# Layer 0's bias sums: three folds by DMA, one product a unit, and VectorE in 2 of 16 evictions

## The chip, the cores and the metric

The kernel runs on one core of one Trainium2 chip. The metric is the device time of one execution in microseconds (us); lower is better. A core has a matrix engine (TensorE, PE in the profile; its weight loads are PEld), a vector engine (VectorE, DVE), an activation engine (ScalarE, ACT), a general engine (GpSimd, POOL) and a queue engine for transfers (SyncE, SP). They run side by side, each in the order of its own instructions, and wait for each other at semaphores. Transfers by DMA are issued from SP's queue, or from GpSimd's, which can also add what it moves to what is there.

## The reference

Four layers run one after the other on x of shape (2, 512, 32, 32), all in float32: a deformable attention with an MLP (layer 0), a linear attention (layer 1) and two full attentions (layers 2 and 3). The change concerns one part of layer 0, the bias of its attention. For each of 16 units (2 batches of 8 groups), each of 1024 queries and each of 64 sampled keys, a small network with 128 hidden channels turns the distance into one number:

```python
pos = grid_q[:, :, None, :] - grid_kv[:, None, :, :]
bias = jnp.sign(pos) * jnp.log1p(jnp.abs(pos))
bias = jax.nn.relu(bias @ cpb_w1 + cpb_b1)
bias = jax.nn.relu(bias @ cpb_w2 + cpb_b2)
bias = (bias @ cpb_w3 + cpb_b3).reshape(b, GROUPS, H * W, Hd * Wd)
sim = jnp.einsum('bhid,bhjd->bhij', qh, kh) + bias
attn = jax.nn.softmax(sim, axis=-1)
```

The last layer of the network is a sum over 128 channels, each weighted by an entry of cpb_w3. Since a positive factor can be moved inside the relu, the kernel scales the second layer's weights by the magnitudes of cpb_w3 and is left with a sum of channels with signs.

## The kernel before, in words

**The loop.** Layer 0 goes through `quads`: unit u (16), set of keys o (8) and half (2), 256 groups in all, numbered i. A group handles 4 keys. `first_hidden` (line 694) has VectorE make the first hidden layer of the next group, i + 1 (line 706). `second_hidden` (line 717) then handles group i in four quarters q of 32 channels. For each quarter, TensorE makes 32 channels of 4 keys on 128 partitions (line 730), so that partition 32k + r holds channel r of key k. ACT evicts it with relu and the bias `magb` (line 740). Quarter 0 holds the channels whose signs may differ from the rest's; ACT multiplies it by `flip` in a second pass (line 742).

**The sum over quarters.** Quarter 0 is added to quarter 1 by an accumulating DMA issued from GpSimd (line 747, 512 KB). GpSimd adds quarter 2 to quarter 3 (line 751). One group later, GpSimd adds the two sums (`join`, line 754, called at q == 1 of the next group's `second_hidden`).

**The folds.** What is left has 32 rows a key. After half 1, the tile `two` holds both halves of an o, and a DMA adds odd partitions to even ones (line 756, 512 KB): 16 rows a key. This goes with the join, one group after half 1. `refold` (line 762) folds a second time to 8 rows a key (line 766, 256 KB) and copies the 32 partitions left of each half into a `sum` tile by two DMAs on SP's queue (line 768, 128 KB each). It is due at group i + 2, where i is the group of half 1 (line 209), and is issued before quarter 3's eviction (line 738), so behind that group's join on GpSimd.

**The products.** Four sets o fill two `sum` tiles, and `sum_product` (line 783, matmul line 786) adds up their rows on TensorE against a matrix of signs into the scores `sim`. So there are two products a unit (`twice_product`, e = 0 and 1), one two sets after each four sets: behind group (u, 5, 1), and behind group (u + 1, 1, 1). There `attend` (line 805) starts for unit u: TensorE adds query times key to `sim` (line 812), and its later parts come one after each group. The end of the last unit has its own treatment (`last_set`), with fewer folds.

**Order and buffers.** PE, ACT, DVE and POOL run in the order in which the program writes the calls (`manual_schedule`, line 147); SP's queue isn't in that list. The quarters' PSUM tiles have 3 buffers (line 135), `two` and `sum` have 3 each (lines 626 to 630), quarters 0, 1 and 2 have 2, 3 and 2 (line 734). `load` (line 643) fetches tables `lb` for the first hidden layer on SP's queue.

Of the kernel before, what the change touches and what calls it, by code (L numbers as in the profile page):

```python
# [11 lines left out]
F32 = mybir.dt.float32  # L12
AF = mybir.ActivationFunctionType
# [22 lines left out]
    ("index", 1), ("row", 1), ("twelves", 8),  # L36
# [12 lines left out]
N_TWICE, N_FOLDED, N_SINGLE = 48, 56, 60  # L49
# [7 lines left out]
class Net:  # L57
# [40 lines left out]
    def layer0(self):  # L98
# [3 lines left out]
        with ExitStack() as ctx:  # L102
# [44 lines left out]
            with self.tc.manual_schedule(engines=engines):  # L147
# [39 lines left out]
                self.join, self.refolds, summed, group, sums = None, [], None, [], []  # L187
                for i, (u, o, half) in enumerate(quads):
# [9 lines left out]
                    last_set = i >= len(quads) - 8  # L198
                    if half == 0:
                        if i + 2 < len(quads):  # L200
                            both = self.two_tiles(f"h2_{u}_{o}3")
                            group.append([both[:, 0, :], both[:, 1, :], both])
                        else:
                            group.append([self.four_rows(f"h2_{u}_{o}{n}3") for n in range(2)])
                        if o % 4 < 2 and not last_set:
                            sums.append(self.four_rows(f"sum{u}_{o}"))
                    self.second_hidden(i, u, o, half, h1, group[-1], i + 1 == len(quads), last_set)
                    if half == 1 and not last_set:
                        self.refolds.append((i + 2, group[-1][2], sums[o % 2], o % 4 // 2))
                    if half == 1 and o % 4 == 1 and summed:  # L210
                        v, e, zs = summed
                        self.twice_product(v, e, zs, sims, ps_s)
                        summed = None
                        if e == 1:
                            if v == 8:
                                self.advance(after, lambda: False)
                                att = [apool.tile([P, N], F32, tag=f"att{t}", name=f"att{v}_{t}") for t in range(CT)]
                            self.advance(front, lambda: "v" in pairs[v // 2])
                            after.append(self.attend(v, pairs[v // 2], sims.pop(v), att, ps))
                            if v % 8 == 7:  # L220
                                after.append(self.projection(ps, att, ow, v // 8))
                    elif half == 1 and o % 4 == 3:
                        if last_set:
                            self.folded_product(u, o - 2, group[:2], sims)
                        else:
                            summed, group, sums = (u, o // 4, sums), [], []
# [5 lines left out]
                self.folded_product(u, o, group[2:3], sims)  # L232
# [35 lines left out]
    def sorted_weights(self, keep):  # L268
# [8 lines left out]
        self.places = self.spare[:, 3 * P : 4 * P + N_TWICE + N_FOLDED + N_SINGLE]  # L277
# [13 lines left out]
        many = keep.tile([P, 8], F32, tag="many", name="sort_many")  # L291
        vec.tensor_tensor(many, self.colr("twelves", 8), total.to_broadcast([P, 8]), ALU.is_le)
        vec.tensor_reduce(c["groups"], many, AX.X, ALU.add)
        vec.tensor_scalar(c["late"], c["groups"], 12.0, None, ALU.mult)
        vec.tensor_scalar(c["rest"], c["groups"], -12.0, 96.0, ALU.mult, ALU.add)
# [16 lines left out]
        signed = keep.tile([P, N_TWICE + N_FOLDED + N_SINGLE], F32, tag="signed", name="signed")  # L312
        pool.tensor_scalar(signed, self.places[:, P:], c["sign"], 1.0, ALU.mult, ALU.mult)
        self.twice = signed[:, 0:N_TWICE]
        self.folded = signed[:, N_TWICE : N_TWICE + N_FOLDED]
        self.single = signed[:, N_TWICE + N_FOLDED :]
# [15 lines left out]
        nc.scalar.copy(self.magb, small)  # L332
        self.flip = keep.tile([P, 1], F32, tag="flip", name="flip")
# [383 lines left out]
    def second_hidden(self, i, u, o, half, h1, one, final, last_set):  # L717
# [4 lines left out]
        nc = self.nc  # L722
        ys = []
        for q in range(4):
# [8 lines left out]
            if q < 3:  # L733
                y = self.hid2.tile([P, N], F32, tag=f"h2{q}", bufs=(2, 3, 2)[q], name=f"h2_{u}_{o}{half}{q}")
            else:
                y = one[half]
                if self.refolds and self.refolds[0][0] <= i:
                    self.refold(*self.refolds.pop(0)[1:])
            ys.append(y)
            nc.scalar.activation(y, hp, AF.Relu, bias=self.magb[:, q, 0:1])  # L740
            if q == 0:
                nc.scalar.activation(y, y, AF.Copy, scale=self.flip)  # L742
            elif q == 1:
                if final:
                    nc.vector.tensor_tensor(y, y, ys[0], ALU.add)
                else:
                    nc.gpsimd.dma_start(y, ys[0], accum_op=ALU.add)  # L747
                if self.join:
                    self.join(final)
            elif q == 3:  # L750
                (nc.vector if final else nc.gpsimd).tensor_tensor(y, y, ys[2], ALU.add)  # L751

        def join(final, z=ys[3], other=ys[1], fold=half == 1 and not final):
            (nc.vector if final else nc.gpsimd).tensor_tensor(z, z, other, ALU.add)  # L754
            if fold:
                nc.gpsimd.dma_start(one[2][0::2], one[2][1::2], accum_op=ALU.add)  # L756
                if last_set:
                    nc.sync.dma_start(one[0][1::2, :], one[1][0::2, :])
# [3 lines left out]
    def refold(self, both, to, second):  # L762


        nc = self.nc
        nc.gpsimd.dma_start(both[0::4], both[2::4], accum_op=ALU.add)  # L766
        for half in range(2):
            nc.sync.dma_start(to[2 * second + half :: 4, :], both[0::4, half, :])

    def twice_product(self, u, e, zs, sims, ps_s):  # L770

        if u not in sims:
            sims[u] = ps_s.tile([P, HF], F32, tag="sim", name=f"sim{u}")
        at = 16 - 16 * e
        self.sum_product(u, self.twice[:, at : at + 32], e == 0, zs, sims)

    def folded_product(self, u, o, group, sims):
        at = 24 - 4 * (o - o % 2)  # L780
        self.sum_product(u, self.folded[:, at : at + 32], False, [one[0] for one in group], sims)

    def sum_product(self, u, lhsT, start, zs, sims):
        for h in range(2):
            for jj, z in enumerate(zs):
                self.nc.tensor.matmul(
                    sims[u][h * NJ + jj * 32 : h * NJ + jj * 32 + 32, :],
# [1250 lines left out]
def _places():  # L2038

    q, row = np.arange(P) // 32, np.arange(P) % 32  # L2040
    got = np.zeros((P, P + N_TWICE + N_FOLDED + N_SINGLE), np.float32)
    got[:, :P] = np.where(q == 0, 96 + row, 12 * (row // 4) + 4 * (q - 1) + row % 4)
    p = np.arange(P)
    got[p, P + 16 + 8 * (p // 2 % 2) + 4 * (p % 2) + p // 32] = 1
    got[p, P + N_TWICE + 24 + 4 * (p % 2) + p // 32] = 1
    got[p, P + N_TWICE + N_FOLDED + 28 + p // 32] = 1
    return got


def _layout(i):  # L2050
# [10 lines left out]
    def over(v):  # L2061
        return np.broadcast_to(v.reshape(1, -1), (P, v.size))
# [12 lines left out]
        "row": (np.arange(P) % 32 // 4).astype(np.float32).reshape(P, 1), "twelves": over(np.arange(12, 108, 12, dtype=np.float32)),  # L2075
# [46 lines left out]
```

## Time and profile before

| | |
|---|---|
| median of 3 runs | 3221.99 us (3221.45 to 3223.23) |
| profiled execution, its own time | 3223.45 us |
| span from first to last instruction | 3221.7 us |
| granted TensorE clock, mean | 1.000 |
| PE busy | 3206.4 us (100%) |
| DVE busy | 2365.0 us (73%) |
| ACT busy | 1958.2 us (61%) |
| POOL busy | 2359.2 us (73%) |
| POOL DMA issues: line 747, 756, 766 | 255, 127, 124 |

All times of the profile are of one execution. A group line gives the line of the program, the engine and the operation, what it writes and reads by the program's names, the shape and the count; then busy time in us and the mean of one in ns; then the engine's idle time just before, and what ended it. Slices are fortieths of the span, each digit a share in tenths. In a timeline the columns are start, length, engine and line. "DMA to landing" is the time from a transfer's issue until its semaphore says that it has arrived. Layer 0's groups take about the first 1900 us.

### The profile page before, as it was taken

To read this page: it belongs to the slowest core of one execution; us is meant where nothing else is said; L and a number is where in the kernel's file an instruction comes from. 1 tells how busy PE (TensorE), PEld (TensorE's weight loads), DVE (VectorE), ACT (ScalarE), POOL (GpSimd) and SP (SyncE) were. 2 spreads that over 40 slices of the span, in tenths; PEclk is the share of its full clock that TensorE was granted. 3 is DMA by queue.
4 is the path that set the end of the run, shared out by engine and by line. 5 is a ranking of instruction groups with operands and counts; after the bars stand their busy time and mean duration, and the time that the engine had idled before them with its cause. 6 is when DMAs were issued, how large, how long until landed. Compare 5 with 4: busy or idle time off the path is not lost.

```text
span 3221.7 us, 58840 instructions
## 1 busy us (share of the span) xinstructions
PE 3206.4 (100%) x24188; PEld 1218.9 (38%) x24188; DVE 2365.0 (73%) x2746; ACT 1958.2 (61%) x2032; POOL 2359.2 (73%) x1558
## 2 busy tenths in 40 slices
PE   9999999999999999999999999999999999999999
PEld 4343333333333333333333334444555433455333
DVE  7778788778777778878777765475475689755897
ACT  7887887887886687887887752112231566213662
POOL 6999999999998699998999964442343458634575
PEclk9999999999999999999999999999999999999999
DMA  6787877787786577777787762111000000000001
GB/s 178 163 172 158 171 168 163 166 167 165 162 172 145 124 164 161 163 163 164 163 174 160 166 166 79 39 40 39 1 1 12 29 1 1 15 1 14 1 2 54
DMA packets 94350, 341.90 MB, mean 106 GB/s; under 512 B 16624, under 2 KB 18800, under 8 KB 78896
## 3 DMA queue, kind: packets, MB, share of 16 engines
q0 software_dynamic: 52832, 232.82, 37.4%
q1 hardware_dynamic: 40224, 103.06, 10.0%
q8 instruction: 195, 3.19, 0.4%
q10 hardware_dynamic: 1008, 2.08, 0.2%
q14 instruction: 91, 0.75, 0.1%
HBM read 67.36 MB, written 4.46 MB: 22 GB/s over the span
## 4 chain that ended last, share of the span: by engine, by line
PE 90%; DVE 5%; POOL 2%; DMA 1%; issue 1%; ACT 0%; DVEq 0%; SPq 0%; POOLq 0%; ACTq 0%
PE hp L730 52%; PE s L1659 5%; PE o L1688 5%; PE qk20P L1434 2%; PE qk30P L1434 2%; PE qk31P L1434 1%; PE m_7P L943 1%; PE m_6P L943 1%; PE m_4P L943 1%; PE m_3P L943 1%; PE m_0P L943 1%; PE qk21P L1434 1%; PE m_5P L943 1%; PE m_2P L943 1%; PE m_1P L943 1%; DVE sum L1675 1%
## 5 line engine op out<-in xcount | busy, mean ns | idle before, releaser
L730 PE MATMUL hp<-h,w2s 128*32 128x512 f32 x16384 | 1784.1, 593 | 0.2
L706 DVE CUSTOM_DVE_ANT_1 h<-tx,bank 128x1024 f32<-128x1024 f32 (+1 forms) x1028 | 1180.9, 1211 | 295.7 <-PE hp L730 197.6
L740 ACT ACTIVATE h<-hp,magb 128x1024 f32<-128x1024 f32 x1024 | 1131.2, 1109 | 359.6 <-PE hp L730 357.7
L730 PEld LDWEIGHTS hp<-h,w2s 128*32 128x32 f32 x16384 | 559.3, 110 | 1187.0 <-issue 1126.4
L754 POOL TENSOR_TENSOR h<-h,h 128x1024 f32<-128x1024 f32 x254 | 728.2, 2867 | 2.4 <-DMA h<-h 2.3
L751 POOL TENSOR_TENSOR h<-h,h 128x1024 f32<-128x1024 f32 x255 | 717.4, 2814 | 1.5 <-ACT h L740 1.5
L1663 ACT ACTIVATE e<-s 128x1024 f32<-128x1024 f32 x256 | 261.8, 1024 | 181.0 <-PE s L1659 176.5
L747 POOL DMA_DIRECT2D h<-h x255 | 275.4, 1080 | 99.6 <-ACT h L740 97.7
L742 ACT ACTIVATE h<-h,flip 128x1024 f32<-128x1024 f32 x256 | 295.0, 1152 | 8.4
L1688 PE MATMUL o<-e,v 64*64 64x512 f32 x2048 | 265.3, 590 | 2.1 <-DVE q L1727 2.1
L1659 PE MATMUL s<-q,k 64*64 64x512 f32 x2048 | 266.0, 591 | 0.0
L1670 POOL TENSOR_TENSOR some<-some,e 128x1024 f32<-128x1024 f32 x64 | 167.6, 2619 | 26.7 <-ACT e L1663 24.1
L1668 POOL TENSOR_TENSOR some<-e,e 128x1024 f32<-128x1024 f32 x32 | 76.1, 2377 | 141.4 <-DVE sum L1677 106.3
L766 POOL DMA_DIRECT2D h<-h x124 | 140.6, 1134 | 27.0 <-DMA h<-h 24.6
L1675 DVE TENSOR_TENSOR sum<-sum,e 128x1024 f32<-128x1024 f32 x64 | 124.0, 1937 | 29.5 <-ACT e L1663 26.8
L913 POOL TENSOR_TENSOR mlp_w<-mlp_w 128x512 f32<-128x512 f32 x16 | 24.2, 1514 | 160.4 <-DMA mlp_w<-in_mlp_w 96.0
L756 POOL DMA_DIRECT2D h<-h x127 | 109.1, 859 | 38.9 <-POOL h L754 37.2
L1688 PEld LDWEIGHTS o<-e,v 64*64 64x64 f32 x2048 | 77.9, 133 | 144.9 <-issue 135.1
L1659 PEld LDWEIGHTS s<-q,k 64*64 64x64 f32 x2048 | 76.5, 133 | 133.2 <-issue 117.2
L1009 ACT ACTIVATE mh<-mh,cols 128x512 f32<-128x512 f32 x64 | 46.0, 721 | 124.4 <-DVE mh L1027 64.3
L1422 POOL TENSOR_TENSOR sq<-q 128x512 f32<-128x512 f32 x32 | 33.2, 1039 | 98.0 <-DVE q L1441 54.3
L1673 DVE TENSOR_TENSOR sum<-e,e 128x1024 f32<-128x1024 f32 x32 | 80.8, 2524 | 32.0 <-ACT e L1663 32.0
(583 smaller groups left out, 3254.4 us busy)
## 6 DMA issues: line engine op xcount, KB each, us to landing
h<-h POOLq DMA_DIRECT2D x382, 512.0 KB, 5.6
lb<-logs SPq DMA_DIRECT2D x63, 512.0 KB, 6.5
h<-h POOLq DMA_DIRECT2D x124, 256.0 KB, 3.7
sum<-h SPq DMA_DIRECT2D x248, 128.0 KB, 3.5
mlp_w<-in_mlp_w SPq DMA_DIRECT2D x16, 1024.0 KB, 4.9
x<-in_x SPq DMA_DIRECT2D x8, 512.0 KB, 7.8
qkw<-in_l_qk SPq DMA_DIRECT2D x2, 2048.0 KB, 7.9
out<-x SPq DMA_DIRECT2D x15, 256.0 KB, 2.1
```

What stands on the lines that cost most here:

```text
L706: self.nc.vector._custom_dve(TENSOR_ADD_SAT, out=h1[r][:, k, cut, :], in0=x[:, 4 * half + 2 * r + k, :].unsqueeze(1).to_broadcast([P, H // ...
L730: nc.tensor.matmul(hp[rows, cut], lhsT=self.l0w2[:, 32 * q : 32 * q + 32], rhs=h1[k][:, cut], start=True, stop=True)
L740: nc.scalar.activation(y, hp, AF.Relu, bias=self.magb[:, q, 0:1])
L742: nc.scalar.activation(y, y, AF.Copy, scale=self.flip)
L747: nc.gpsimd.dma_start(y, ys[0], accum_op=ALU.add)
L751: (nc.vector if final else nc.gpsimd).tensor_tensor(y, y, ys[2], ALU.add)
L754: (nc.vector if final else nc.gpsimd).tensor_tensor(z, z, other, ALU.add)
L943: self.nc.tensor.matmul(acc[p], lhsT=w[:, a, k, p * P : (p + 1) * P], rhs=right(r, k), start=k == 0, stop=k == 1)
L1434: nc.tensor.matmul(acc, lhsT=left[0][a][:, c, t * P : (t + 1) * P], rhs=r[ri][:, c, :], start=c == 0, stop=c == 1)
L1659: nc.tensor.matmul(s[halves[c], par, :], lhsT=ks[p][rows, at : at + DH], rhs=qs[p][rows, cut], start=True, stop=True)
L1663: nc.scalar.activation(e, s, AF.Exp, scale=DH**-0.5)
L1688: nc.tensor.matmul(o[halves[par], r, :], lhsT=v[n // 2][rows, n % 2, at : at + DH], rhs=e[rows, par, :], start=(n == 0), stop=(n == NB - 1),)
```

## The change

- Units 0 to 14 fold a third time: a DMA adds rows 4::8 of `two` to rows 0::8 (16 partitions, 128 KB), leaving 4 rows a key. The two copies on SP's queue then take 16 partitions each (64 KB), and all eight sets of a unit share two `sum` tiles. There is one product a unit, with a new sign matrix `thrice`, at the place where the second one was: behind group (u + 1, 1, 1).
- `refold` becomes a generator. Its first step (the second fold) is due at group i + 2, its second (the third fold and the copies) one group later. `refold_more` makes due steps at q == 1, behind the join. The last unit folds twice, as before (`once`).
- The sorting of channels by sign goes in sets of 24 instead of 12, since the rows left of a key now hold 24 channels of the three last quarters and 8 of the first.
- In groups (3, 0) and (4, 1) of units 1 to 15 (`fused`), VectorE evicts quarter 2 and adds quarter 1 in one instruction: max with `under`, which is minus the bias, plus quarter 1. The bias left out there is added in quarter 0's second pass on ACT. The DMA now adds quarter 0 to quarter 2, after VectorE; GpSimd's addition of quarter 2 to quarter 3 is gone in these groups, and the join adds quarter 2.

```diff
@@ layer0
-                        if o % 4 < 2 and not last_set:
+                        if o < 2:
                             sums.append(self.four_rows(f"sum{u}_{o}"))
                     self.second_hidden(i, u, o, half, h1, group[-1], i + 1 == len(quads), last_set)
                     if half == 1 and not last_set:
-                        self.refolds.append((i + 2, group[-1][2], sums[o % 2], o % 4 // 2))
-                    if half == 1 and o % 4 == 1 and summed:
-                        v, e, zs = summed
-                        self.twice_product(v, e, zs, sims, ps_s)
-                        summed = None
...
+                        self.refolds.append([i + 2, self.refold(group[-1][2], sums[o % 2], o // 2, u == last)])
+                    if half == 1 and o == 1 and u > 0:
+                        v = u - 1
+                        sims[v] = ps_s.tile([P, HF], F32, tag="sim", name=f"sim{v}")
+                        self.sum_product(sims[v], self.thrice, True, before)
...
@@ sorted_weights
+        self.under = keep.tile([P, 1], F32, tag="under", name="under")
+        pool.tensor_scalar(self.under, self.magb[:, 2, 0:1], -1.0, 1.0, ALU.mult, ALU.mult)
@@ second_hidden
+        fused = u > 0 and (o, half) in ((3, 0), (4, 1)) and not final
...
             ys.append(y)
+            if q == 2 and fused:
+                vec.scalar_tensor_tensor(y, hp, self.under, ys[1], ALU.max, ALU.add)
+                pool.dma_start(y, ys[0], accum_op=ALU.add)
+                continue
             nc.scalar.activation(y, hp, AF.Relu, bias=self.magb[:, q, 0:1])
-            if q == 0:
+            if q == 0 and fused:
+                nc.scalar.activation(y, y, AF.Identity, scale=self.flip, bias=self.magb[:, 2, 0:1])
+            elif q == 0:
                 nc.scalar.activation(y, y, AF.Copy, scale=self.flip)
             elif q == 1:
...
-                else:
-                    nc.gpsimd.dma_start(y, ys[0], accum_op=ALU.add)
+                elif not fused:
+                    pool.dma_start(y, ys[0], accum_op=ALU.add)
                 if self.join:
                     self.join(final)
-            elif q == 3:
-                (nc.vector if final else nc.gpsimd).tensor_tensor(y, y, ys[2], ALU.add)
+                self.refold_more(i)
+            elif q == 3 and not fused:
+                (vec if final else pool).tensor_tensor(y, y, ys[2], ALU.add)
 
-        def join(final, z=ys[3], other=ys[1], fold=half == 1 and not final):
+        def join(final, z=ys[3], other=ys[2 if fused else 1], fold=half == 1 and not final):
...
-    def refold(self, both, to, second):
+    def refold_more(self, i):
+
+        going = []
+        for at, fold in self.refolds:
+            if at <= i:
+                for _ in fold:
+                    going.append((at + 1, fold))
+                    break
+            else:
+                going.append((at, fold))
+        self.refolds = going
+
+    def refold(self, both, to, c, once):
 
 
         nc = self.nc
         nc.gpsimd.dma_start(both[0::4], both[2::4], accum_op=ALU.add)
+        if not once:
+            yield
+            nc.gpsimd.dma_start(both[0::8], both[4::8], accum_op=ALU.add)
+        n = 4 if once else 8
         for half in range(2):
-            nc.sync.dma_start(to[2 * second + half :: 4, :], both[0::4, half, :])
+            nc.sync.dma_start(to[2 * c + half :: n, :], both[0::n, half, :])
```

## The prediction

> **What bounds the kernel now.** I read the page first: its slices, chain and groups.
>
> ```profile
> PE   9999999999999999999999999999999999999999
> POOL 6999999999998699998999964442343458634575
> PE 90%; DVE 5%; POOL 2%; DMA 1%; issue 1%; ACT 0%; DVEq 0%; SPq 0%; POOLq 0%; ACTq 0%
> L730 PE MATMUL hp<-h,w2s 128*32 128x512 f32 x16384 | 1784.1, 593 | 0.2
> L754 POOL TENSOR_TENSOR h<-h,h 128x1024 f32<-128x1024 f32 x254 | 728.2, 2867 | 2.4 <-DMA h<-h 2.3
> L751 POOL TENSOR_TENSOR h<-h,h 128x1024 f32<-128x1024 f32 x255 | 717.4, 2814 | 1.5 <-ACT h L740 1.5
> ```
>
> TensorE never rests: 0.2 us of idle time before 16384 matmuls. So one microsecond more or less of TensorE work or waiting in layer 0 is one microsecond of the kernel. GpSimd is the next fullest. Whatever ACT, VectorE or GpSimd are given or spared counts only if TensorE then waits. I write (u, o, half) for a group: unit u, key set o of 8, half 0 or 1; q is its quarter.
>
> So the next question is what TensorE's product L786 waits for, and how close that is. The answer for the copies' line L768 names it:
>
> ```profile
> L768 SPq DMA_DIRECT2D sum<-h x248: 458/524/2575, 60.1 to 1867.2; - x124
> ...
> who waited for it (us, times):
>   PEld sim L786: 1.4, 3
> ```
>
> Three of 31 products already wait a little for the copies of the folded sums. The margin is thin. Here is one product in order of time (start, length), the one at (u,1,1) that the change keeps; first TensorE, then GpSimd:
>
> ```profile
> 844.42 13.94 PE L730 MATMUL hp<-h,w2s 128*32 128x512 f32 x128
> 858.18 1.04 PE L786 MATMUL sim<-sum,signed 128*32 128x512 f32 x8
> ```
>
> ```profile
> 848.00 0.84 POOL L766 DMA_DIRECT2D h<-h  x1 [0.18 <-issue]
> 848.60 2.66 POOL L751 TENSOR_TENSOR h<-h,h 128x1024 f32<-128x1024 f32 x1
> 850.93 1.15 POOL L747 DMA_DIRECT2D h<-h  x1
> 851.54 2.97 POOL L754 TENSOR_TENSOR h<-h,h 128x1024 f32<-128x1024 f32 x1
> 854.81 0.86 POOL L756 DMA_DIRECT2D h<-h  x1 [0.29 <-POOL h L754]
> 857.75 1.14 POOL L747 DMA_DIRECT2D h<-h  x1
> ```
>
> The two groups (1,0) and (1,1) run from 844.4 to 858.2. The second fold L766 of the previous unit's o=7 goes out at 848.00, in the order written for (0,1). Asked for L766 and L768 in the stretches round it, the trace gives 3.4 us to landing for the fold, and for its two copies, issued from 851.50:
>
> ```profile
> DMA to landing us min/median/max: 3.0/3.7/4.4
> ```
>
> The second copy went out at 852.05 and took 4.4 us: the sums were whole at 856.4, 1.8 us before the product's place at 858.18.
>
> **What the Trainium skill says.** "DMA: Bandwidth & Descriptors", section "Queues, rings and completion order": descriptors are consumed in ring order on each DMA engine. So a fold issued straight behind another of the same queue waits for the other's data. The trace agrees as far as it goes: GpSimd's folds of 256 KB land after 3.7 us and those of 512 KB after 5.6 (medians), so more bytes ahead mean a later landing. Its section "Anatomy of one DMA — SWDGE (gpsimd) path" gives about 2.0 us fixed plus the bytes; this kernel's fastest fold took 3.2, so I use the trace. "TensorE: Matmul & The Clock Gate", section "Part 1: The HAM clock gate": TensorE falls to half rate after a free-running window of about 3.4 us without work, and needs about 3.4 us of work to come back. Here the longest gap before the end is 1.6 us, so no stretch of layer 0 shows it. The end of the trace does (columns: stretch, its length, busy time and count of PE, PEld, DVE, ACT and POOL, the clock, DMA share, GB/s):
>
> ```profile
> 3217.20:3219.90 2.70, 0.00 (x0) 0.00 (x0) 0.48 (x1) 0.00 (x0) 0.00 (x0) 1.00 0.56 188
> 3219.90:3221.70 1.80, 0.00 (x0) 0.00 (x0) 0.00 (x0) 0.00 (x0) 0.00 (x0) 0.50 0.02 7
> ```
>
> The clock is 0.50 from 2.7 us after the last matmul.
>
> **Part by part.**
>
> *Products.* Before, each unit ends in two products, after o=3 and after o=7. The change keeps one for units 0 to 14; unit 15 keeps what it had. The chain of waits shows 0.86 us for one (8 records at 858.36). Removed: 15 x 0.86 = 12.9 us of TensorE, on the path. **-12.9 us.**
>
> *The third fold, its issue.* 15 units x 8 = 120 more GpSimd DMAs. From the start of L747 at 850.93 to the next operation is 0.6 us; 8 x 0.6 = 4.8 us a unit. Removed from GpSimd: the q3 addition L751 in two groups of units 1 to 15, 2 x 2.8 = 5.6 us a unit. In the unit from 743.0 to 858.6 GpSimd is busy 107.5 of 115.6 us. It stays about there: 0 us, under TensorE's cover.
>
> *The third fold, its date.* This is the term that decides. The generator issues the second fold at group i+2 and the third, with the copies, at i+3, in both cases behind that group's join. For o=7 that is (1,0) of the next unit, and the product stays behind (1,1). In the stretch above, GpSimd reaches that point after L747, L754 and the first fold L756 of 854.81, thus at 854.81 + 0.6 = 855.4. TensorE's place for the product is 858.18: 2.8 us for a fold, a wake-up of SP and two copies. Now the price:
> - L756 of 854.81 landed after 4.4 us, at 859.3. The third fold is 128 KB behind it in the same queue. From 256 KB to 512 KB the stretch shows 3.4 and 4.4 us, so 0.5 us for 128 KB: 859.8. Low end: not held behind it, 3.2 us (the fastest L766) from 855.4: 858.6.
> - SP answers a landing in 0.1 us (landed 851.44, issued 851.50). Each copy is now 64 KB instead of 128. At 864.54 an undisturbed pair was whole 2.6 us after its first issue; the median pair takes 4.8 us. The bytes are half, but L747 of 857.75 moves its data then (it landed after 4.8 us). I take the middle, 3.6: 863.5.
> - So the product waits 863.5 - 858.2 = 5.3 us. Over the 15 products at this place the trace has 3.8 us on average from L756's issue to the product and 4.9 us to L756's landing: 4.9 + 0.5 + 0.1 + 3.6 - 3.8 = 5.3 again. Ends: 3.1 (no queueing, short copies) and 6.5 (median pair of before).
> TensorE issues in order, so attention's products of that unit and group (2,0) stand behind it. Nothing is won back: it had no idle time to give. 15 x 5.3 = **+79.5 us.**
>
> *The clock.* A gap of 5.3 us holds a whole free-running window of 3.4 us in (5.3 - 3.4)/3.4 = 0.56 of cases; the return at half rate costs half of 3.4 us. 0.56 x 1.7 x 15 = **+14 us**, an estimate from the skill's page; ends 0 and 15 x 1.7 = 25.
>
> *VectorE's eviction.* In (3,0) and (4,1) VectorE does max and add from PSUM. The nearest row is L375, also PSUM plus SBUF to 128x1024: 1.29 us, against ACT's 1.11 for the eviction it spares. Behind it on VectorE stands the next first hidden layer, 4.6 us of a 6.9 us group; the attention's steps leave VectorE nothing else in these two groups (one has the exponential on ACT, the other copies on ACT). TensorE needs the bank two quarters, 3.4 us, later. 0 us; if that cover is gone, up to 1 us x 30. The accumulating DMA now waits for VectorE instead of ACT's q1, some 1 to 2 us later; the join that needs it is a group later and may make GpSimd wait as long: within its slack.
>
> *The folded tiles.* There are three of `two`, and a tile of o is rewritten by q3 of (o+3,0). Copies whole at 863.5 stand against ACT's eviction near 867; over the trace the median time for the copies is 4.7 us and a fifth have under 3.5. ACT would then wait about 1 us, and TensorE has 2 us of spare banks. 0 us; bound +15.
>
> *SP.* The copies wait on SP's queue some 7 us longer. The loads of `lb` share it, but they go out a whole table (28 us) early. 0 us. Setup and `under`: below 0.5 us, taken as 0.
>
> Sum: -12.9 + 79.5 + 14 = +80.6 us on the profiled execution's 3223.45 us (span 3221.70, and 1.75 around it). That execution is 1.46 us over the median of 3221.99; on the median: 3222 + 81 = **3303 us**.
>
> **The rivals.**
> - *A short stall* (0.15). The third fold overtakes, the clock stays: 15 x 3.1 - 12.9 = +34, 3256 us. For it: small transfers have landed in 1.9 us. Against it: the fold goes out 0.6 us behind a 512 KB one.
> - *A long stall* (0.18). Copies no faster than now, clock down each time, tiles late: 15 x 6.5 + 25 + 15 - 12.9 = +125, 3347 us. For it: the copies' median is 3.5 us with a maximum of 11.3.
> - *The other side, sums in time* (0.04). Only the 12.9 us of products count: 3209 us. One mechanism: the third fold and its copies fit into the 2.8 us before the product. It decides where the chain from fold to last copy is under 2.8 us; from 3.7 us up even the saved product is lost. No fold of the trace lands under 3.2 alone. A still smaller chance (0.02) lies between.
>
> **How the numbers follow.** Main case 0.61 at 3303, with 3280 to 3330 as its own range; the rivals as above. The range of 3256 to 3345 leaves out some 2 in 10: the short stall's lower half, the long one's upper part, the other side. Faster by over 0.2% (6.4 us, about what a measurement can tell) 0.04, within 0.2% 0.02, slower 0.94.
>
> **What would show it.** TensorE's idle time before L786's successor in the new code should be 4 to 6 us in 15 places, put down to the copies sum<-h; the product's matmuls halve from 248 recorded to about 128. Matmuls after the gap should be slow for about 3 us if the clock falls. GpSimd's busy share should hold. I am wrong if the copies land before TensorE gets there, or if the waits on ACT or GpSimd grow beside the product.

## The result, and the profile after

| | before | after |
|---|---|---|
| median | 3222.44 us (3221.45 to 3223.23, 4 runs) | 3440.14 us (3434.46 to 3446.85, 4 runs) |
| span of the profiled execution | 3221.7 us | 3445.1 us |
| PE busy | 3206.4 us | 3268.7 us |
| TensorE idle in the span | 15.3 us | 176.4 us |

The ratio is 1.0677, with a 95% interval from 1.0657 to 1.0696. The kernel is 218 us slower; 81 were predicted. The direction was right, and the time lies 95 us above the range.

The page of the changed kernel first: busy times, two rows of slices, and the chain.

```profile
PE 3268.7 (95%) x24068; PEld 1203.3 (35%) x24068; DVE 2402.7 (70%) x2776; ACT 1911.0 (55%) x2002; POOL 2377.2 (69%) x1649
...
PE   9998988998999999989889989999999999999999
...
POOL 7978978878878688789789786434234357734576
...
PE 38%; POOL 36%; issue 10%; DMA 9%; DVE 5%; ACT 1%; SPq 0%; POOLq 0%; ACTq 0%; DVEq 0%
```

The row of nines has holes, all in the first 24 slices, which is layer 0. The chain that was 90% TensorE is now 38% TensorE, 36% GpSimd and 9% transfers. But GpSimd isn't full: its slices stand mostly at 7 and 8 where they stood at 9. No engine is busy throughout layer 0; they wait for each other. The groups say where:

```profile
L738 PE MATMUL hp<-h,w2s 128*32 128x512 f32 x16384 | 1839.2, 601 | 73.5 <-ACT h L750 69.9
...
L767 POOL TENSOR_TENSOR h<-h,h 128x1024 f32<-128x1024 f32 x254 | 744.9, 2933 | 119.2 <-DMA h<-h 118.4
...
L805 PE MATMUL sim<-sum,signed 128*32 128x512 f32 x128 | 43.8, 881 | 86.2 <-DMA sum<-h 80.1
```

L805 is the product (L786 before), L738 the second layer's matmul (L730 before, with 0.2 us idle), L767 the join. The product's group before had no idle time:

```profile
L786 PE MATMUL sim<-sum,signed 128*32 128x512 f32 x248 | 33.9, 593 | 0.0
```

After, TensorE has idled 86.2 us before products and 73.5 us before L738, the latter behind ACT's evictions L750. The waits of the whole trace name what ACT waited for (columns: total, times, longest):

```profile
ACT h L750 <- DMA sum<-h: 138.0, 43, 7.4
POOL h L767 <- DMA h<-h: 118.4, 30, 5.6
ACT h L750 <- DMA h<-h: 92.7, 35, 5.6
PE sim L805 <- DMA sum<-h: 80.1, 14, 9.9
PE hp L738 <- ACT h L750: 69.9, 56, 5.1
```

The first line is the tile `two`: quarter 3 of a group (o+3, 0) can't be written while copies still read it. In this execution 37 of its 43 waits stand at (0,0), (5,0), (6,0) and (7,0). The third line is mostly quarter 0's tile, which the transfer of VectorE's groups still reads: 26 of its 35 waits, 69 of its 92.7 us, stand at quarter 0 of (4,0) and (5,1), two groups behind VectorE's.

Four numbers make up all but 1.6 us of the difference of the spans, 223.4 us: products saved -12.9 (the prediction's price of 0.86 us each); gaps at products +86; gaps before L738, nearly all behind ACT, +73 (73.5 less 0.2); and PE's busy time, which rose by 62.3 although 12.9 us of products are gone, so +75. What stretched it is for the most part the clock. Here is one pause in stretches (start and end, length, busy time and count of PE, PEld, DVE, ACT, POOL, the granted clock, DMA share, GB/s):

```profile
780.00:788.27 8.27, 8.27 (x80) 2.28 (x72) 8.07 (x9) 4.49 (x5) 8.27 (x7) 1.00 0.86 160
788.27:790.30 2.03, 0.00 (x1) 0.00 (x0) 2.03 (x2) 1.17 (x2) 2.03 (x3) 1.00 0.18 32
790.30:791.40 1.10, 1.10 (x12) 0.42 (x16) 0.12 (x1) 1.07 (x2) 1.10 (x1) 1.00 0.96 186
791.40:794.81 3.41, 3.41 (x20) 0.87 (x16) 0.00 (x0) 3.04 (x3) 3.12 (x4) 0.50 0.80 154
794.81:796.60 1.79, 1.79 (x40) 1.01 (x32) 0.00 (x0) 0.89 (x1) 1.79 (x3) 1.00 1.26 201
```

TensorE pauses for 2.03 us. Then 1.1 us later, when it is at work again, the clock falls to 0.50 for 3.41 us: 20 matmuls in 3.41 us there, where the first row has 80 in 8.27 us. (Of the 40 in the last row, 32 are smaller ones of another line.) Layer 0 has 27 such stretches of 3.41, 6.83 or 10.24 us, 136.5 us together. TensorE is busy in 100.3 us of them, so half speed costs 50 us. The other 25 of the 75 aren't the clock's; e18, below, has such a rise at full clock. A part is the way of counting: in this trace four matmuls of 0.59 us start every 0.43 us, so the last ones before a pause still count as busy while nothing new starts. That gives 0.16 us for each of layer 0's 79 pauses of over 0.15 us, some 13 us, as an estimate. The rest I can't assign.

The product's place is one example of how the sums are late (start, length, engine, line; a bracket is the wait before):

```profile
827.34 1.07 POOL L794 DMA_DIRECT2D h<-h  x1
...
832.78 1.56 SPq L797 DMA_DIRECT2D sum<-h  x2
...
836.16 1.07 PE L805 MATMUL sim<-sum,signed 128*32 128x512 f32 x3 [3.81 <-DMA sum<-h]
```

The third fold goes out at 827.34; SP issues the copies at 832.78, 5.4 us later; the product starts 3.4 us after that. In the same unit, a tile:

```profile
792.91 1.07 POOL L794 DMA_DIRECT2D h<-h  x1
...
802.11 0.37 SPq L652 DMA_DIRECT2D lb<-logs  x1
802.64 31.70 SPq L797 DMA_DIRECT2D sum<-h  x6
...
810.41 2.12 ACT L750 ACTIVATE h<-hp,magb 128x1024 f32<-128x1024 f32 x2 [7.16 <-DMA sum<-h]
811.58 5.34 PE L738 MATMUL hp<-h,w2s 128*32 128x512 f32 x32 [4.42 <-ACT h L750]
```

Here the copies also queue on SP behind a load of `lb`, which leaves at 802.11. ACT waits 7.16 us for the tile, and TensorE pauses 4.42 us behind ACT. A group of VectorE:

```profile
860.95 1.28 DVE L747 SCALAR_TENSOR_TENSOR h<-hp,under,h 128x1024 f32<-128x1024 f32 x1
...
862.83 0.86 POOL L769 DMA_DIRECT2D h<-h  x1 [0.29 <-POOL h L767]
...
863.42 1.07 POOL L794 DMA_DIRECT2D h<-h  x1
...
863.92 1.48 POOL L748 DMA_DIRECT2D h<-h  x1
...
871.38 1.11 ACT L750 ACTIVATE h<-hp,magb 128x1024 f32<-128x1024 f32 x1 [2.00 <-DMA h<-h]
...
871.43 2.40 POOL L767 TENSOR_TENSOR h<-h,h 128x1024 f32<-128x1024 f32 x1 [3.88 <-DMA h<-h]
```

VectorE is done at 862.2. Its transfer L748 leaves at 863.92, behind the first fold L769 and the third fold L794 in GpSimd's queue, and arrives only at about 871.4. The join waits 3.88 us, and ACT's quarter 0 waits 2.00 us for the tile that L748 reads.

### The profile page after: what moved, and what is told of

Its sections match the earlier page's. It is cut to its first block, busy times and chain, and to the rows that moved or that the text cites. A ratio compares the mean times of both kernels' runs of the same rounds, so it can differ in the third digit from the quotient of the medians.

```text
span 3445.1 us, 58749 instructions
## 1 busy us (share of the span) xinstructions
PE 3268.7 (95%) x24068; PEld 1203.3 (35%) x24068; DVE 2402.7 (70%) x2776; ACT 1911.0 (55%) x2002; POOL 2377.2 (69%) x1649
## 4 chain that ended last, share of the span: by engine, by line
PE 38%; POOL 36%; issue 10%; DMA 9%; DVE 5%; ACT 1%; SPq 0%; POOLq 0%; ACTq 0%; DVEq 0%
POOL h L767 15%; POOL h L764 9%; DMA h<-h 6%; POOL h L759 6%; PE s L1678 5%; PE o L1707 5%; PE hp L738 4%; DMA sum<-h 2%; POOL h L791 2%; POOL tx L654 2%; POOL h L769 1%; PE qk20P L1453 1%; PE qk30P L1453 1%; POOL h L794 1%; PE m_0P L962 1%
## 5 line engine op out<-in xcount | busy, mean ns | idle before, releaser
L738 PE MATMUL hp<-h,w2s 128*32 128x512 f32 x16384 | 1839.2, 601 | 73.5 <-ACT h L750 69.9
L750 ACT ACTIVATE h<-hp,magb 128x1024 f32<-128x1024 f32 x994 | 1082.5, 1109 | 622.8 <-PE hp L738 389.7
L738 PEld LDWEIGHTS hp<-h,w2s 128*32 128x32 f32 x16384 | 546.7, 111 | 1324.3 <-issue 1099.2
L767 POOL TENSOR_TENSOR h<-h,h 128x1024 f32<-128x1024 f32 x254 | 744.9, 2933 | 119.2 <-DMA h<-h 118.4
L759 POOL DMA_DIRECT2D h<-h x225 | 315.8, 1404 | 201.2 <-ACT h L750 201.1
L754 ACT ACTIVATE h<-h,flip 128x1024 f32<-128x1024 f32 x226 | 260.1, 1151 | 7.4
L791 POOL DMA_DIRECT2D h<-h x124 | 178.3, 1438 | 0.5 <-DMA h<-h 0.5
L769 POOL DMA_DIRECT2D h<-h x127 | 108.8, 856 | 41.3 <-POOL h L767 36.7
L932 POOL TENSOR_TENSOR mlp_w<-mlp_w 128x512 f32<-128x512 f32 x16 | 23.6, 1473 | 159.7 <-DMA mlp_w<-in_mlp_w 114.3
L794 POOL DMA_DIRECT2D h<-h x120 | 127.2, 1060 | 2.2 <-DMA h<-h 1.1
L805 PE MATMUL sim<-sum,signed 128*32 128x512 f32 x128 | 43.8, 881 | 86.2 <-DMA sum<-h 80.1
```

Source lines behind the costliest of these rows:

```text
L738: nc.tensor.matmul(hp[rows, cut], lhsT=self.l0w2[:, 32 * q : 32 * q + 32], rhs=h1[k][:, cut], start=True, stop=True)
L759: pool.dma_start(y, ys[0], accum_op=ALU.add)
L767: (vec if final else pool).tensor_tensor(z, z, other, ALU.add)
```

## The experiments

My theory after this reading: one thing costs the time, the date at which the folded sums arrive. It shows at the product, at the tile, and, by most pauses of 2 us or more, in the clock. The rivals were the load of 120 more transfers, whatever their place, and VectorE's groups. Each expectation uses its own letters for what it tells apart. Times are medians; the kernel before ran beside each at about 3222 us. `fused = False` below means that ACT evicts everywhere.

**e1: without VectorE's groups.**

```diff
-        fused = u > 0 and (o, half) in ((3, 0), (4, 1)) and not final
+        fused = False
```

> The changed kernel with VectorE's eviction switched off in all groups (fused = False): GpSimd adds quarter 2 again, three folds and one product a unit stay. Theory A (the third fold comes too late for the product and for the tiles that it leaves late; VectorE's groups add nothing of their own): ACT goes on waiting for the copies sum<-h, the time stays above 3400 us. Theory B (a good part of ACT's and GpSimd's waits comes from the accumulating DMA of the two VectorE groups, which is issued behind the folds and lands after 7 us): only the wait of the product and its clock stay, 3222 - 13 + 86 + some 45 = about 3340 us, and the waits of ACT on sum<-h nearly go.

3398.66 us, ratio 1.0544 (1.0513 to 1.0575). That is close to theory A, just under its bound: ACT still waits 125.0 us for the copies. VectorE's groups cost 41 of the 218 us in this company. The join's wait is gone (0.0 us). The other two groups stay large:

```profile
L738 PE MATMUL hp<-h,w2s 128*32 128x512 f32 x16384 | 1829.8, 600 | 52.3 <-ACT h L750 51.9
...
L805 PE MATMUL sim<-sum,signed 128*32 128x512 f32 x128 | 43.5, 875 | 71.5 <-DMA sum<-h 65.9
```

**e2: the change with its product one group later.**

```diff
-                    if half == 1 and o == 1 and u > 0:
+                    if half == 0 and o == 2 and u > 0:
```

> The changed kernel with the unit's product and what follows it (attention of that unit) one group later, behind (2,0) instead of (1,1). Theory A: the product's wait of 86 us and the half clock after it (some 90 of 136 us at half rate, worth 45) go, about 3310 us remain, with ACT's waits for tiles as they are. Rival C (the waits are one lag of GpSimd and DMA that TensorE must pay somewhere; without the pause at the product it pays at ACT): the waits on ACT grow by as much, the time stays above 3400 us.

3331.78 us, ratio 1.0337 (1.0307 to 1.0367): half of the loss goes with one line. TensorE's gaps at the product fall from 86.2 to 21.5 us, and the half-speed stretches from 136.5 to 41.0 us; TensorE is busy in 35.4 us of these, so the clock costs 18 us instead of 50. The gaps before L738 are still 55.2 us, and ACT's waits for the copies grow from 138.0 to 183.4 us. The time is 22 us above theory A's 3310.

**e3: the kernel before, made to wait.** The same kind of wait without any part of the change: both products of a unit moved one group earlier than their sums.

```diff
-                    if half == 1 and o % 4 == 1 and summed:
+                    if half == 0 and o % 4 == 1 and summed:
```

> The kernel before, with both products of a unit one group earlier, behind half 0 of the key set instead of half 1. Nothing else changes: two folds, no VectorE eviction. It makes TensorE wait about 5 us (6.9 us of a group less the margin of about 1.8) at 31 places and so prices a pause by itself. If a pause costs its length alone: 3222 + 31 x 5.1 = 3380 us. If the clock falls only when a whole window of 3.4 us lies in the pause, as I had taken it: + 31 x 0.5 x 1.7 = 26 us, 3405. If every pause brings the clock down for one to three windows (6 us at half rate on average, 3 us lost), as the changed kernel's trace suggests: 3380 + 93 = about 3470 us.

3414.57 us, ratio 1.0593 (1.0563 to 1.0624). Its busy times, and the product's group:

```profile
PE 3283.5 (96%) x24188; PEld 1320.2 (39%) x24188; DVE 2362.0 (69%) x2746; ACT 1957.2 (57%) x2032; POOL 2359.6 (69%) x1558
...
L786 PE MATMUL sim<-sum,signed 128*32 128x512 f32 x248 | 80.4, 813 | 114.3 <-DMA sum<-h 80.3
```

The pauses are 114.3 us in 30 places, 3.8 each where 5.1 were expected. PE's busy time rises by 77.1 us with the same work. So a pause of this length costs its own 3.8 us and 2.6 us more. Of the 77.1 us the clock explains 45: there are 109.2 us at half speed, with TensorE busy in 90.2 of them. This shows the clock's cost apart from the change, 1.5 us a pause; the other 32 us I can't assign.

**e5: VectorE's groups alone, in the kernel before.** Edit: `under`, `fused` and its branches, no third fold.

> The kernel before with VectorE's eviction of quarter 2 in groups (3,0) and (4,1) of units 1 to 15, and nothing else of the change: two folds, two products. If these groups cost by themselves (accumulating DMA issued after VectorE, behind the fold, its landing awaited by GpSimd's join and by ACT): 3222 + 20 to 40 us. If they cost only together with the third fold in the queue ahead of them: within 6 us of 3222, since GpSimd's 8 us of idle time a unit cover the join's wait.

3238.35 us, ratio 1.0052 (1.0029 to 1.0074): +16 us, without a third fold in the way, between the two cases that I had set apart. The join's group:

```profile
L763 POOL TENSOR_TENSOR h<-h,h 128x1024 f32<-128x1024 f32 x254 | 708.8, 2791 | 70.1 <-DMA h<-h 69.3
```

The join waits 70.1 us here and 119.2 us in the changed kernel, where two folds can stand ahead of the transfer.

**e9: the transfers' issue alone.** The kernel before with a further transfer of 128 KB behind each first fold (127 of them, not 128) from GpSimd, into memory that nothing reads.

```diff
                 nc.gpsimd.dma_start(one[2][0::2], one[2][1::2], accum_op=ALU.add)
+                aside = self.dram.tile([P // 8, 2, N], F32, tag="aside", name=f"aside_{u}_{o}")
+                nc.gpsimd.dma_start(aside, one[2][1::8])
```

> The kernel before plus one transfer a key set that nobody waits for: GpSimd issues, right behind the first fold, a plain DMA of 16 partitions (128 KB) of the folded tile to memory, 128 in all. It is the third fold's issue without its dates. If an issue costs GpSimd 0.6 us, as I had taken it: 4.8 us a unit within 8 us of idle time, the time stays within 5 us of 3222. If it costs its whole row of 1.1 to 1.4 us (the addition behind it is slowed too): 9 to 11 us a unit against 8, GpSimd falls behind TensorE in each unit and the time rises by 15 to 60 us.

3235.47 us, ratio 1.0041 (1.0022 to 1.0061). GpSimd's idle time before its transfers of L747 and the second fold falls from 99.6 + 27.0 to 62.2 + 12.4 us, 0.4 us for each added transfer. So the load alone isn't the 218 us; these 13 us are with 5.6 us of waiting at a product.

**e4, e6, e7: the third fold earlier in the same pair of groups.** In e4 it follows quarter 3's addition of the second fold's own group; in e6 and e7 it stands at the head of the next group, ahead of L759 (quarter 1's transfer) and the join. No VectorE groups; the product is late in e4 and e7. The first call below is that of e6 and e7, the second that of e4, behind quarter 3's addition.

```diff
+            if q == 0:
+                self.refold_more(i - 0.5)
...
+                self.refold_more(i + 0.5)
...
-                    going.append((at + 1, fold))
+                    going.append((at + 0.5, fold))
```

> The changed kernel without VectorE's eviction, with the third fold and the copies in the same group as the second fold (behind quarter 3 instead of one group later), and the product behind (2,0). If lateness of the third fold is the whole cause: no wait of TensorE is left and only the saved products count, 3222 - 13 = 3209 us. If the third fold's 120 issues and landings make GpSimd or the DMA queue the bound (GpSimd is at 107.5 of 115.6 us a unit before): above 3230 us, with ACT or TensorE waiting for GpSimd.

> The changed kernel without VectorE's eviction, with the third fold still one group after the second but at that group's start, ahead of L747, the join and the first fold, instead of behind them. Product at its place behind (1,1). Theory A (the fold is late because it stands behind 4 us of GpSimd's work and in the queue behind the 512 KB of the first fold): it goes out about 4 us earlier and lands in 3.3 us instead of 5.9, so the sums are whole 6 to 7 us earlier, the product waits 0 to 1.5 us, and ACT no longer waits for sum<-h: 3215 to 3250 us. If GpSimd is the bound with 120 more issues: above 3300 us with waits on L747's DMA, as where the third fold followed in the same group.

> As the one before, and the product behind (2,0). Theory A: no wait of TensorE left, the saved products show, 3209 us, which beats the kernel before. If the bound is GpSimd: not below 3230 us.

3400.79, 3368.67 and 3401.25 us (ratios 1.0551, 1.0456, 1.0557). The fold itself lands in 3.1 us in all three, where it took 5.5 (medians). Yet all three times lie far above what an early fold was to give. e6 gains 30 us against e1, but e4 and e7 lose 102 against e15 below (3299.59 us), which differs from them in the late fold alone. The waits of e4 show why:

```profile
ACT h L750 <- DMA h<-h: 398.5, 161, 6.6
POOL h L796 <- DMA h<-h: 153.5, 87, 4.4
PE hp L738 <- ACT h L750: 127.6, 146, 4.5
```

L796 is the third fold. It now reaches the head of GpSimd's queue before the second fold has landed and waits there, 153.5 us in 87 places, with quarter 1's transfers and the joins behind it. ACT then waits for the tiles. In e6 the product, left in its place, still waits 64.6 us. An early place has to be one where what it needs is already there.

**e8, e10, e11, e12: VectorE in other groups.** e10 is e7 with VectorE's two groups; e8 has only (3,1), e11 has (3,1), (5,1), (6,1) and (7,1); e12 has these four with the fold where the change put it and the late product.

> As the one before, with VectorE's eviction in one group a unit, (3,1), where the later attention leaves VectorE free and no third fold is issued. If GpSimd has become the bound, the 2.8 us a unit that it is spared show: faster than the one before by some 20 to 40 us. If TensorE bounds: the same within 3 us; if the late accumulating DMA costs: slower by 10 us or more.

> The changed kernel with VectorE's two groups as they are, the third fold at the start of its group (ahead of L747 and the first fold), and the product behind (2,0). GpSimd is spared 5.6 us a unit against the run without VectorE's groups, which took 3401 us with ACT waiting for L747's DMA. If GpSimd's load is the bound there: 3330 us or less. If the fused groups' own DMA is what costs: 3380 us or more.

> As the one before, with VectorE's eviction in four groups a unit, all with half 1: (3,1), (5,1), (6,1), (7,1), where neither the first nor the third fold is issued ahead of their DMA. GpSimd is spared 11.2 us a unit, about what the eight third folds cost it. If its load is the bound: no wait longer than a microsecond is left, 3209 to 3225 us, perhaps below the kernel before. If the later DMA of each such group costs more than GpSimd gains: above 3300 us, with ACT's and the join's waits on DMA h<-h.

> The same four groups and the product behind (2,0), but the third fold one group after the second behind join and first fold, as in the changed kernel. Against e2 (3332 us): GpSimd has 5.6 us a unit less to do, the fused DMA is no longer behind two folds. If the third fold's late landing still holds ACT's quarter 3 (waits on sum<-h of about 130 us in the middle of layer 0): 3280 to 3340 us; if these waits came from GpSimd's lag: below 3250 us.

In this order, e8, e10, e11 and e12 took 3386.03, 3416.30, 3402.71 and 3405.95 us (ratios 1.051, 1.0604, 1.0561, 1.0572). I had hoped that a GpSimd spared of additions would keep up with the early fold. In e10 and e11 the other side came true, that the later transfers cost; e8 and e12 fit neither of their sides. The head-of-queue wait stays (170.5 us in e11), and more VectorE groups add join waits (234.9 us in e12). None comes near e2.

**e15, e16, e14: the tile.** e15 is e1 with the late product. e16 is e15 with a fourth `two` tile, paid for by one `sum` tile and one of quarter 1's. e14 has the four tiles, but the product in the change's place.

```diff
-        return self.hid2.tile([P, 2, N], F32, tag="two", bufs=3, name=name)
+        return self.hid2.tile([P, 2, N], F32, tag="two", bufs=4, name=name)
```

> The changed kernel without VectorE's eviction and with four tiles two instead of three (room from sum, 3 to 2, and quarter 1, 3 to 2). Product at its place. Against e1 (3399 us, 52 us of TensorE's waits behind ACT): if these come from the tile that the third fold leaves late, they go, and 3222 - 13 + 72 of the product's waits + 40 of its clock = about 3320 us remain. If they are GpSimd's lag, ACT waits for another tile instead: above 3380 us.

> e1 with the product behind (2,0): no VectorE groups, third fold as in the change. Theory: e1's 72 us of product waits and their clock go, ACT's waits for the tile stay or grow, since TensorE's pause no longer lets the folds catch up: 3300 to 3350 us. If the pause at the product was what kept GpSimd in step: 3380 us or more.

> Both of the last two: four tiles two, and the product behind (2,0). If the product and the tile are the two places, and the only ones, where the third fold's date meets TensorE: 3209 to 3225 us. If GpSimd with 120 more issues is slower than TensorE: above 3250 us, with ACT waiting for L747's DMA.

e15 3299.59 (1.0241, 1.0212 to 1.0271), e16 3269.28 (1.0147, 1.0118 to 1.0177), e14 3372.08 (1.0466, 1.0436 to 1.0497). In e14 and e16 ACT's waits for the copies are gone, and the gaps before L738 fall from 52.3 (e1) to 7.6 us and from 44.9 (e15) to 5.1: the tile was their cause. e15 came out just under the lower end of its range. e14 lies between what its two sides gave. e16 misses the 3209 to 3225 us: even the late product still waits 25.2 us there. And these two groups of e14 show what else happens:

```profile
L738 PE MATMUL hp<-h,w2s 128*32 128x512 f32 x16384 | 1810.6, 595 | 7.6 <-ACT h L750 7.1
...
L805 PE MATMUL sim<-sum,signed 128*32 128x512 f32 x128 | 45.3, 918 | 103.1 <-DMA sum<-h 103.1
```

Against e1 the gaps behind ACT fell by 45 us and those at the product grew by 32. A TensorE that isn't stopped on the way comes to its product earlier and waits there. The two waits partly hide each other.

**e13: the fold behind the join but ahead of the first fold.** No VectorE groups, late product, three tiles. The move's core:

```diff
                 if self.join:
                     self.join(final)
-                self.refold_more(i)
...
         def join(final, z=ys[3], other=ys[2 if fused else 1], fold=half == 1 and not final):
...
+            self.refold_more(i + 1)
```

> The changed kernel without VectorE's eviction, the third fold in its own group and behind the join, but issued ahead of the first fold of the next key set instead of behind it, and the product behind (2,0). The second fold has landed by then, so GpSimd has nothing to wait for, and the third fold doesn't stand behind 512 KB in the queue (3.1 to 3.3 us to landing instead of 5.9). If lateness in the queue and waits at the head of GpSimd's order are the cause: no wait of ACT for sum<-h and none of the product, 3209 to 3225 us. If GpSimd or the queue can't carry a third fold at all: above 3300 us.

3278.12 us, ratio 1.0175 (1.0145 to 1.0204). The second and third fold both stay behind a join, but the third no longer queues behind 512 KB: it lands after 4.1 us. Against e15 that gains 21 us, but 3209 to 3225 were expected. The gaps before L738 only fall from 44.9 to 36.9 us; for o=5 a load of `lb` holds the copies on SP in 11 of the 15 units, as shown above for one.

**e17 and e18: all mends together.** e17 is e13 with e16's tiles; e18 adds VectorE's groups again.

> Here the third fold of before's fourth-row scheme keeps its arithmetic, ACT evicts everywhere, the third fold is issued behind the join but ahead of the first fold, the product comes one group later, at (u+1,2,0), and there are four folded tiles and two sum tiles. Theory A (only the dates of fold, copies and tiles cost time; each mend takes away its own part): the tile waits of e13 (30 us of pauses plus some 25 us of half clock) and the product's waits of e16 (25 us plus 12 of clock) both go, a few microseconds of start-up stay: 3210 to 3230 us, TensorE's gaps before the end under 10 us. Theory B (120 more transfers crowd GpSimd's and SP's queues whatever their place): 20 us or more of gaps stay, and the time is 3245 us or more.

> As e17, with VectorE's two groups a unit put back. Theory A (they spare GpSimd 5.6 us a unit but make its joins wait as long): within 10 us of e17. Theory B (their late transfer behind the folds decides, as e1 and e5 showed singly): 16 to 41 us above e17, with join waits of 50 us or more and pauses of TensorE behind ACT.

e17: 3222.50 us (12 runs), ratio 1.0001 (0.9992 to 1.0010). Its page:

```profile
PE 3200.1 (99%) x24068; PEld 1202.6 (37%) x24068; DVE 2374.8 (74%) x2746; ACT 1956.3 (61%) x2032; POOL 2447.4 (76%) x1679
...
L738 PE MATMUL hp<-h,w2s 128*32 128x512 f32 x16384 | 1783.2, 593 | 4.3 <-ACT h L750 3.5
...
L805 PE MATMUL sim<-sum,signed 128*32 128x512 f32 x128 | 17.8, 593 | 0.7 <-DMA sum<-h 0.7
```

This takes all of the 218 us away. Each of the last two mends is large by itself: the order of the folds brings e16's 3269 us down by 47, and the tiles bring e13's 3278 down by 56. The rival that 120 more transfers must cost some 200 us wherever they stand has fallen: they are all here, and the kernel is as fast as before. But it isn't faster, though it has 12.9 us of products less. (The products' row is 16.1 us shorter, 33.9 to 17.8; it overlaps its neighbours.) TensorE's idle time is 4.8 us longer (20.1 for 15.3). In the setup there are 6.8 us at half clock, which I can't explain; they cost 3.4, and L738 starts 2.8 us later behind them (25.9 for 23.1). e14, e16 and e18, the other kernels with four `two` tiles, show both as well. Some 3 us are left unassigned.

e18: 3274.24 us, ratio 1.0158 (1.0141 to 1.0175), 52 us above e17. I expected either under 10 or 16 to 41: both were too low. Two of its waits:

```profile
ACT h L750 <- POOL h L766: 134.9, 124, 2.5
POOL h L766 <- DMA h<-h: 125.3, 30, 5.3
```

The join L766 waits 4.2 us in each of VectorE's 30 groups. With two tiles for quarter 1 instead of three, ACT then waits for the join directly. So part of the 52 us belongs to the tiles given away; I didn't separate them. The clock stays at full speed in layer 0's groups here: only one pause reaches 2.1 us. Even so PE's busy time is 24.3 us longer than e17's, with the same work:

```profile
PE 3224.4 (98%) x24068; PEld 1220.6 (37%) x24068; DVE 2409.4 (74%) x2776; ACT 1917.6 (59%) x2002; POOL 2373.8 (73%) x1649
```

e18 has 63 pauses of over 0.15 us in layer 0 where e17 has 10. So a pause adds to the busy time without the clock too, here about 0.46 us each.

## Why the prediction was wrong, step by step

- **Products, -12.9: right in its kind.** The product records fall from 248 to 128. No run shows the saving by itself: e17, which has it, is not faster than the kernel before.
- **The third fold's date, +79.5: right.** The gaps are 86.2 us in 15 places, 5.75 each for 5.3. The working behind it was off in one term: the fold of o=7 lands 5.5 us after its issue in the mean, not 4.4, while its copies took 3.4 for 3.6. That is 0.9 us more of a chain, and half of it shows at the product. The closeness is in part luck, since TensorE's stops at the tiles, which I hadn't counted, shorten the wait at the product: in e14, nearly without these stops, it is 103.1 us, where e1 has 71.5. The medians that I read as a sign of queueing, 3.7 us for 256 KB and 5.6 for 512 KB, compare a fold's own bytes, not those ahead of it. Only the runs show the queue's part: 5.9 us behind the first fold in e15, 4.1 ahead of it in e13.
- **The clock, +14 with an end of 25: mis-sized.** It cost about 50 us. I took from the Trainium skill, "TensorE: Matmul & The Clock Gate", Part 1, that TensorE falls to half rate after an idle window of about 3.4 us, and so counted only the share of pauses that hold one whole, at 1.7 us each. The runs disagree. In the changed kernel all 19 pauses of layer 0 between 0.8 and 1.93 us left the clock alone; of five from 2.03 to 2.26 us three brought it down, and all 24 longer ones did. A window needn't be idle whole: some 2.0 us of idle time in one were enough, as the last section works out. The clock also stayed down for up to 10.24 us instead of 3.4. e3, which has nothing of the change, gives 1.5 us of clock for each pause of 3.8 us, where my rule gives 0.2. The kernel before had a hint at its end, in the lines that the prediction shows: the clock fell 2.7 us after the last matmul, before 3.4 were full.
- **The folded tiles, 0 with a bound of 15: the step that failed most.** I wrote that ACT would wait about 1 us, and TensorE had 2 us of banks. ACT waited 138 us in 43 places, up to 7.4, and TensorE's gaps before L738 came to 73.5 us with VectorE's share (52.3 without it, e1). I held the tile against one chain, 4.4 + 3.6, with 3.5 us to spare, and used a median where the late tail decides: fold landings reach 8.4 us and copies 7.2. e14 and e16 show the cause by taking it away.
- **VectorE's eviction, 0: half right.** The instruction takes 1.28 us (1.29 predicted), and nothing waits long for VectorE. Wrong was the sentence that the join's wait lies "within its slack": the transfer was moved behind the join's own folds in GpSimd's queue, arrives 7.4 us after its issue, and holds both GpSimd and a tile of quarter 0. Removing the groups gives 41 us back (e1); alone they cost 16 (e5), and beside the mends 52, the tiles given away included (e18).
- **GpSimd's issue, 0: right as a price.** 0.6 us each was taken, e9 shows 0.4. In e17, with the same span as before, GpSimd's busy time is 88 us longer for 120 transfers, 0.7 each, its slower additions included.
- **SP, 0: nearly.** In the changed kernel's 15 copies of o=5, four were held 1.7 to 4.4 us behind a load of `lb`; the loads don't always go out "a whole table (28 us) early".

The range missed because the clock and the tiles, both nearly left out, come from one mechanism. I treated the late fold as 15 waits at one place, but the fold comes 120 times, and each time it also holds a tile. My long-stall rival had all three terms (clock, tiles, stall) in it, and priced the first two at 40 us where, with VectorE's share, they came to some 125, and to 150 with the busy time that stays unassigned. The sign that I had named for being wrong, waits on ACT that grow beside the product, is what came.

## What to carry to other kernels

When a step is moved later, follow its data to every reader and every buffer it holds, at each of its places and with the late tail of its transfers, not only to the product that it feeds. On a TensorE-bound kernel a pause costs more than its length, above all where some 2 us of it fall into one of the clock's windows, so price it from a measured pair of pause and busy time. In an in-order queue, a transfer belongs behind what it needs and ahead of larger transfers that others don't wait for; moving it ahead of what it needs stalls everything behind it.

## What the runs showed of the hardware that I had not expected

- Pauses of TensorE between 2.0 and about 3.6 us brought the clock down in some places and not in others: of e3's eleven pauses from 2.44 to 3.57 us six left it up, all 18 longer ones brought it down. What decides is where a pause lies. In each trace the half-speed stretches between 40 and 2150 us all start on one grid with steps of 3.41 us, to within 0.01 us. I counted the steps of the 16 traces that have such stretches. A step at full speed in which TensorE was idle for more than 2.02 us was always followed by half speed, and one with less than 1.95 us never was (221 falls in some 9500 steps). Two cases of it: the changed kernel's pause of 2.03 us at 788.27 lies in one step, and the clock fell; e3's pause of 3.57 us at 1411.8 lies across an edge, 1.88 and 1.69 us, and it didn't. The way back is decided near 0.8 us: the clock rose after steps with up to 0.79 us of idle time, and stayed down after those from 0.78 us on.
- The copies with half the bytes were hardly faster: those of 64 KB took 3.4 us where those of 128 KB took 3.5 (medians). The place in the queue mattered more: the same third fold of 128 KB landed after 5.5 us behind the first fold, 4.1 ahead of it (e13, e17), and 3.1 at the head of a group (e6).
- GpSimd's additions of the same shape became longer in most kernels with the third fold: 2814 ns at quarter 3 and 2867 at the join before, 3145 and 3114 in e17, but only 2902 and 2944 in e7, with the third fold at the head of a group. e9, with 127 added transfers that go to another memory and add nothing up, has 2849 and 2928. I didn't find the cause.
